# Weighted context as [token, feature] instead of [feature, token] in a gated cross-attention block

## The chip, the cores and the metric

The kernel runs on one core of one Trainium2 chip. The metric is the device time of one execution in microseconds; the time before is the median of three runs. Engine names in the profile: PE is TensorE (PEld its weight loads), DVE VectorE, ACT ScalarE, POOL GpSimd, SP SyncE, which issues most transfers.

## What is computed

Eight sequences (B = 8) of 512 tokens with 256 features attend to 1024 context rows of 192 features each. Per head (4 heads of 32) the 32 largest scores of a token are kept, their softmax is the attention row, and the mean over the heads weighs the context:

```python
Q = (x_text @ Wq).reshape(Bb, Tt, H, DH)
K = (x_vision @ Wk).reshape(Bb, Gg, H, DH)
scores = jnp.einsum('bthd,bghd->bhtg', Q, K) / np.sqrt(DH).astype(np.float32)
topv, topi = jax.lax.top_k(scores, K_TOP)
probs = jax.nn.softmax(topv, axis=-1)
attn = jnp.zeros_like(scores).at[bi, hi, ti, topi].set(probs)
attn_mean = attn.mean(axis=1)
V = x_vision @ Wv
c_t = jnp.einsum('btg,bgd->btd', attn_mean, V)
```

c_t then scales and shifts (FiLM) the normalised tokens ahead of and behind a state-space layer (a long convolution, done as a Fourier transform by matrix products); layer norms, a GELU MLP, and a mixture of a shared expert and one of eight routed experts follow. The kernel folds Wv into the FiLM weights, so that what the attention has to deliver is u = attn_mean @ context, 192 features per token.

## The kernel before

**Tiles.** P = 128, NT = 4 token tiles per batch, NG = 8 groups of 128 context rows, DK = 96 (half of the 192 context features), D = 256. All matrices here are float32. Each batch's context lies in SBUF as `s.cx` [128 rows of a group, 8 groups, 192 features], from a pool with two buffers for that tile, so the load of a batch's context (`prepare`, line 432) waits until the context two batches earlier has been read for the last time.

**Attention** (`attention`, line 907) steps through batch, token tile and pair of heads. A step takes the scores from TensorE (pS), copies them by ScalarE (sc), finds the threshold by VectorE (mn, hi, top), exponentiates, masks and normalises, and GpSimd adds the heads into `acc` [128 tokens, 1024 context rows]. When a token tile's four heads are done, `weighted` (line 871) is left for the next step (`behind`), where it is called after the first half of that step's work.

**`weighted`**, per token tile: eight transposes bring acc to `aT` [context row, group, token] by two banks of PSUM (pa) and two copies by ScalarE. Then for each half k of the features, eight products accumulate over the groups into a third bank (pu): the context's 96 columns are the weights in the array, the tile's 128 tokens stream. The result is [96 features, 128 tokens] for each half, side by side in one bank, and one ScalarE copy takes both halves to `s.uT` [feature, half, token]. `film` (line 1032) later uses uT as the weights of its own products, pfi at the start of `mixed` and pfo at its end.

**Order.** Nothing is issued as it is called. The calls are noted as operations with a modelled cost (`Plan.time`), and `Plan.order` (line 220) simulates the five queues and picks for each engine, among what can begin, the operation with the lowest place in program order. That place is shifted: attention's operations by `LEAD_A` = -100, which puts them behind others, the scores forward again by `LEAD_S` = 300. PSUM banks of the tag "mm" (`bank`, line 397; four of them) and SBUF buffers are granted in program order when one comes free (`grant`, line 243). So a change in one operation's cost, or one more bank, can change the order of everything after it. The streams are interleaved: attention of batch b runs beside `mixed` and `after_mix` of batch b - 1 and the preparation of batch b + 1; routed expert blocks (pxb, pg, pu<-xbT, pyr) are set between. After the last attention tile the last batch's remaining stages and the rest of the expert blocks run alone. The name pu appears twice in the profile: pu<-aT,cx is the weighted context, pu<-xbT,rt_up an expert's product.

**Setting.** `weighted` is called 32 times in the path that runs; a second path for masked rows (`attention_masked`) holds a call too, under a condition that the inputs here don't meet.

Of the kernel before, what the change touches and what calls it, by code (L numbers as in the profile page):

```python
# [12 lines left out]
F32 = mybir.dt.float32  # L13
# [9 lines left out]
P = 128  # L23
# [320 lines left out]
def tile_kernel(ctx: ExitStack, tc: tile.TileContext, a: dict, out: bass.AP):  # L344
# [8 lines left out]
    NE, _, NI = a["L0_ffn_rt_gate"].shape  # L353
    NT, NG, DK = T // P, G // P, DV // 2
# [26 lines left out]
    pk = ctx.enter_context(tc.tile_pool(name="pk", bufs=2))  # L381
# [9 lines left out]
    V, S, GP, TE, SY = (plan.engine(n, e) for n, e in (  # L391
        ("DVE", nc.vector), ("ACT", nc.scalar), ("POOL", nc.gpsimd), ("PE", nc.tensor), ("SP", nc.sync)))
# [4 lines left out]
    def bank(name, pool=ps_mm, tag="mm"):  # L397
        return pool.tile([P, 512], F32, tag=tag, name=name)
# [9 lines left out]
    ident = const.tile([P, P], F32, name="ident")  # L408
# [462 lines left out]
    def weighted(b, s, t, acc):  # L871

        aT = pa.tile([P, NG, P], F32, tag="aT", name=f"aT{b}_{t}")
        for q in range(NG // 4):
            p_ = bank(f"pa{b}_{t}_{q}")
            for i in range(4):
                g = 4 * q + i
                TE.transpose(p_[:, i * P : (i + 1) * P], acc[:, g * P : (g + 1) * P], ident)
            S.copy(aT[:, 4 * q : 4 * q + 4, :].rearrange("p g t -> p (g t)"), p_)
        p_ = bank(f"pu{b}_{t}")  # L880
        for k in range(2):
            for g in range(NG):
                TE.matmul(p_[:DK, k * P : (k + 1) * P], s.cx[:, g, k * DK : (k + 1) * DK],
                          aT[:, g, :], start=(g == 0), stop=(g == NG - 1))
        S.copy(s.uT[:DK, :, t * P : (t + 1) * P],
               p_[:DK, : 2 * P].rearrange("p (k t) -> p k t", k=2))

# [19 lines left out]
    def attention(states):  # L907
# [5 lines left out]
        for k, (b, t, h0) in enumerate(steps):  # L913
# [72 lines left out]
            if h0 + 2 == H:  # L986
                behind = partial(weighted, b, s, t, acc)
# [3 lines left out]
    def attention_masked(b, s):  # L991
# [3 lines left out]
        for t in range(NT):  # L995
            acc = pk.tile([P, G], F32, tag="acc", name=f"acc{b}_{t}")
            for h in range(H):
# [29 lines left out]
                else:  # L1027
                    V.scalar_tensor_tensor(acc, sc, sm[:, 3:4], acc, ALU.mult, ALU.add)
            weighted(b, s, t, acc)


# [396 lines left out]
    p_ = bank("p_ok")  # L1428
# [4 lines left out]
    with tc.If(rows_ok < P):  # L1433
# [10 lines left out]
        for b in range(B):  # L1444
            s = St()
# [51 lines left out]
```

## Time and profile before

| | |
|---|---|
| median of 3 runs | 1786.56 us (1785.48 to 1790.18) |
| the profiled execution | 1792.2 us, span 1790.5 us |
| TensorE busy | 1517.7 us, 85% of the span |
| VectorE busy | 1302.9 us, 73% |
| ScalarE busy | 1154.7 us, 64% |
| GpSimd busy | 929.5 us, 52% |
| mean granted TensorE clock | 0.873 |
| pu<-aT,cx products | 1024 instructions, 116.0 to 1557.9 us, 136.5 us busy |
| first copy to uT, last | 121.3 us, 1558.3 us |

A row of the groups gives the engine and operation, the tile written and those read, for a product the partitions * weight columns, then the shape of the moving operand and the number of instructions; behind the bar the busy time in us and the mean duration of one in ns; behind the next bar the idle time just before, and what ended it. Products are pipelined: a row's mean duration is longer than the distance between two starts. In a busy table each engine has its busy us and the instructions in that stretch; then follow the granted clock (1.00 is full rate), the share of the DMA engines and GB/s. Nearly all instructions carry line 323, the place where the planned order is issued, so groups are told apart by their tiles.

### The profile page before, as it was taken

How to read it: one execution, taken by the hardware profiler on the slowest of the kernel's cores; microseconds unless marked ns; L12 is line 12 of the kernel's file. 1: busy time of each engine (PE TensorE's matmuls, PEld its weight loads, DVE VectorE, ACT ScalarE, POOL GpSimd, SP SyncE). 2: the span in 40 equal slices, each digit the busy share in tenths (PEclk: the TensorE clock that was granted, in tenths of full speed). 3: DMA queues.
4: the chain of work that ended last, by engine and by line, in shares of the span. 5: the costliest groups of instructions: out<-in, count | busy, mean ns of one | idle time of the engine just before them, and what ended most of it. 6: DMA issues, size and time to landing. Idle time of an engine off the chain costs nothing. (4 is left out here: it accounts for less than half of the span.)

```text
span 1790.5 us, 21072 instructions
## 1 busy us (share of the span) xinstructions
PE 1517.7 (85%) x6363; PEld 893.1 (50%) x6363; DVE 1302.9 (73%) x3076; ACT 1154.7 (64%) x2008; POOL 929.5 (52%) x1072
## 2 busy tenths in 40 slices
PE   5365577797998798999889999998999989969995
PEld 2143333344543454474436554654466447637795
DVE  5999977886878697977798889687978798231210
ACT  4778844676747774887578877885788568312321
POOL 5578543445363645565554755574557555432222
PEclk8555677786998799998989999998999899989998
DMA  4000110001200120143103330432033204653592
GB/s 118 0 1 24 33 36 18 12 12 47 64 25 12 47 65 18 36 127 95 56 12 101 89 111 12 130 110 61 12 102 103 80 1 133 206 176 118 162 304 70
DMA packets 101288, 131.67 MB, mean 74 GB/s; under 512 B 9687, under 2 KB 73004, under 8 KB 101166
## 3 DMA queue, kind: packets, MB, share of 16 engines
q1 hardware_dynamic: 93102, 121.05, 21.1%
q0 software_dynamic: 7008, 8.42, 2.6%
q8 instruction: 52, 0.85, 0.2%
q10 hardware_dynamic: 1056, 0.79, 0.2%
q14 instruction: 70, 0.57, 0.1%
HBM read 112.22 MB, written 18.78 MB: 73 GB/s over the span
## 5 line engine op out<-in xcount | busy, mean ns | idle before, releaser
L323 PE MATMUL pS<-kT,qT 32*128 32x512 f32 x512 | 287.7, 748 | 71.0 <-DVE mn L323 60.6
L323 POOL TENSOR_TENSOR acc<-acc,e 128x1024 f32<-128x1024 f32 x96 | 229.1, 2386 | 184.4 <-ACT e L323 181.8
L323 DVE MAX8 top<-mn 128x8 f32<-128x256 f32 (+1 forms) x512 | 276.0, 556 | 11.9
L323 ACT COPY sc<-pS 128x512 f32<-128x512 f32 x256 | 145.6, 584 | 174.3 <-PE pS L323 143.7
L323 DVE SCALAR_TENSOR_TENSOR e<-sc,t,e 128x1024 f32<-128x1024 f32 x128 | 180.9, 1426 | 40.9 <-ACT e L323 40.6
L323 DVE TENSOR_TENSOR mn<-sc,pS 128x512 f32<-128x512 f32 x256 | 165.2, 677 | 36.0 <-PE pS L323 19.9
L323 POOL TENSOR_TENSOR mn<-mn 128x256 int32<-128x256 int32 x128 | 102.5, 801 | 167.5 <-DVE hi L323 166.8
L323 PEld LDWEIGHTS pS<-kT,qT 32*128 32x128 f32 x512 | 76.5, 210 | 204.8 <-DVE mn L323 98.6
L323 ACT ACTIVATE e<-sc,sm 128x1024 f32<-128x1024 f32 x128 | 145.1, 1146 | 15.9 <-POOL acc L323 13.0
L323 ACT ACT_TABLE_LOAD x118 | 151.4, 1283 | 4.1 <-issue 2.0
L323 PE MATMUL pm<-hT,w 128*128 128x512 f32 x256 | 135.9, 668 | 13.5 <-ACT hT L323 13.5
L323 ACT ACTIVATE junk<-sc,sm 128x1024 bf16<-128x1024 f32 x128 | 146.0, 1141 | 1.3
L323 PEld LDWEIGHTS pu<-aT,cx 128*96 128x96 f32 x1024 | 123.2, 169 | 28.6 <-issue 24.1
L323 PE MATMUL pu<-aT,cx 128*96 128x128 f32 x1024 | 136.5, 283 | 0.2 <-ACT aT L323 0.2
L323 PE MATMUL am<-w,ga 128*128 128x256 f32 x512 | 129.1, 398 | 6.1 <-ACT ga L323 6.1
L323 PEld LDWEIGHTS am<-w,ga 128*128 128x128 f32 x512 | 96.9, 196 | 51.4 <-issue 27.6
L323 POOL TENSOR_TENSOR yf<-yf,t 128x512 f32<-128x512 f32 (+1 forms) x80 | 85.9, 1112 | 46.1 <-DVE t L323 45.0
L323 ACT ACTIVATE e<-e,sm 128x1024 f32<-128x1024 f32 x96 | 108.5, 1147 | 1.7 <-DVE sm L323 1.6
L323 POOL TENSOR_TENSOR mn<-mn,hi 128x256 int32<-128x256 int32 x128 | 104.8, 819 | 8.0
L323 DVE MATCH_REPLACE8 mn<-top,mn 128x256 f32<-128x256 f32 x256 | 104.6, 409 | 0.0
L323 PEld LDWEIGHTS pm<-hT,w 128*128 128x128 f32 x256 | 52.1, 213 | 79.2 <-issue 54.2
L323 DVE TENSOR_REDUCE hi<-mn 128x256 f32<-128x512 f32 x128 | 87.9, 687 | 0.0
(303 smaller groups left out, 3073.5 us busy)
## 6 DMA issues: line engine op xcount, KB each, us to landing
w<-in_L_xattn_W_dram SPq DMA_DIRECT2D x32, 512.0 KB
rt_gate<-in_L_ffn_rt_gate_dram SPq DMA_DIRECT2D x30, 512.0 KB
rt_up<-in_L_ffn_rt_up_dram SPq DMA_DIRECT2D x30, 512.0 KB
rt_down<-in_L_ffn_rt_down_dram SPq DMA_DIRECT2D x30, 512.0 KB
cx<-in_ctx_dram SPq DMA_DIRECT2D x7, 768.0 KB
xtab<-zt SPq DMA_DIRECT2D x8, 642.5 KB
xt<-in_x_dram SPq DMA_DIRECT2D x8, 512.0 KB
xo<-in_x_dram SPq DMA_DIRECT2D x8, 512.0 KB
```

What stands on the lines that cost most here:

```text
L323: o.fn()
```

## The change

The products of `weighted` exchange their operands: the tile's attention weights aT [context row, token] become the weights in the array (128 columns), and all 192 features of the context stream at once, so that one chain of eight products gives u as [token, feature] in one bank. ScalarE copies u to SBUF (a new tile of 192 columns with one buffer). Two transposes then turn the two halves of 96 features into a further bank (put), and the copy to `s.uT` is as before. The eight transposes of acc and their copies stay.

```diff
             S.copy(aT[:, 4 * q : 4 * q + 4, :].rearrange("p g t -> p (g t)"), p_)
+
         p_ = bank(f"pu{b}_{t}")
+        for g in range(NG):
+            TE.matmul(p_[:, : 2 * DK], aT[:, g, :], s.cx[:, g, : 2 * DK], start=(g == 0), stop=(g == NG - 1))
+        u = pk.tile([P, 2 * DK], F32, tag="u", name=f"u{b}_{t}", bufs=1)
+        S.copy(u, p_[:, : 2 * DK])
+        p_ = bank(f"put{b}_{t}")
         for k in range(2):
-            for g in range(NG):
-                TE.matmul(p_[:DK, k * P : (k + 1) * P], s.cx[:, g, k * DK : (k + 1) * DK],
-                          aT[:, g, :], start=(g == 0), stop=(g == NG - 1))
+            TE.transpose(p_[:DK, k * P : (k + 1) * P], u[:, k * DK : (k + 1) * DK], ident)
         S.copy(s.uT[:DK, :, t * P : (t + 1) * P],
                p_[:DK, : 2 * P].rearrange("p (k t) -> p k t", k=2))
```

## The prediction

> **What bounds the kernel now.** First the page's busy times and granted clock, then the busy table for three stages that I chose: filter set-up beside the first attention tiles, the steady part, and the tail after the last attention tile.
>
> ```profile
> PE 1517.7 (85%) x6363; PEld 893.1 (50%) x6363; DVE 1302.9 (73%) x3076; ACT 1154.7 (64%) x2008; POOL 929.5 (52%) x1072
> ```
>
> ```profile
> core 0: us, PE busy (x) PEld busy (x) DVE busy (x) ACT busy (x) POOL busy (x), PEclk, DMA share, GB/s
> 100.00:500.00 400.00, 300.52 (x1275) 162.12 (x1276) 325.98 (x707) 274.92 (x463) 216.02 (x197) 0.73 0.09 29
> 500.00:1560.00 1060.00, 981.56 (x3878) 563.73 (x3877) 854.20 (x2104) 769.06 (x1334) 597.99 (x724) 0.94 0.23 71
> ```
>
> From 500 to 1560 us TensorE is busy 93% of the time and no other engine is above 81%: the steady part is TensorE's queue plus its waits. From 100 to 500 VectorE leads (81%) and the clock is granted 0.73. The longest waits of TensorE in the steady part:
>
> ```profile
> PE pc L323 <- DMA cx<-in_ctx_dram: 15.9, 3, 6.2
> PE pm L323 <- ACT hT L323: 12.8, 6, 5.0
> PE pyr L323 <- DVE ger L323: 11.0, 7, 3.1
> PE hT_p L323 <- ACT hh L323: 10.2, 5, 3.8
> ```
>
> All of its waits there add up to about 78 us. So work taken from TensorE counts, unless one of these waits grows by as much. Then the groups that the change touches, or that price what it adds:
>
> ```profile
> L323 PE MATMUL pu<-aT,cx 128*96 128x128 f32 x1024 | 136.5, 283 | 0.2 <-ACT aT L323 0.2
> L323 PEld LDWEIGHTS pu<-aT,cx 128*96 128x96 f32 x1024 | 123.2, 169 | 28.6 <-issue 24.1 <-ACT aT L323 2.2 <-ACT junk L323 1.0
> L323 PE MATMUL pc<-ident,cx 128*96 128x128 f32 x128 | 24.0, 338 | 33.5 <-DMA cx<-in_ctx_dram 33.5
> L323 ACT COPY uT<-pu 96x256 f32<-96x256 f32 x32 | 11.6, 363 | 31.4 <-PE pu L323 31.4
> L323 ACT COPY ktime<-pz 32x128 f32<-32x128 f32 x32 | 8.1, 253 | 10.3 <-PE pz L323 10.1
> ```
>
> A float32 product is two instructions here (32 tiles x 16 products = 512, and 1024 rows), a transpose is one (pc, 128 of them). Means overlap, so costs are taken from starts in TensorE's timeline: at full clock 32 instructions of pu run from 1087.29 to 1090.78, 3.49 us, 109 ns each. Eight of pm with 512 columns take 3.43 us (timeline, 1626.37 to the next row at 1629.80): 429 ns, 0.84 ns a column. A pu instruction is thus its 128 columns (107 ns) and 2 ns more; the weight load is hidden.
>
> **The change, part by part.**
>
> *Products.* Removed per tile: 32 x 109 = 3.49 us. Added: 8 products x 2 instructions x 192 columns x 0.84 = 16 x 161 = 2.58 us. Fewer columns stream, because 192 columns fill the moving side where 96 of 128 array columns were used. Weights now have 128 columns instead of 96, but there are half as many loads; pg with 128-column weights and 128 moving columns takes 1.79 us for 16, 112 ns, so a 128-column load already hides under 112 ns and will under 161. I count 0 for it; if the cover failed, 3 ns x 16 x 32 = 1.5 us in all.
>
> *Two transposes per tile,* nearest row pc (same 96 x 128 shape): 2 x 109 = 0.22 us. TensorE net: 3.49 - 2.58 - 0.22 = 0.69 us saved per tile at full clock, double at half clock.
>
> *The copy of u,* PSUM to SBUF, 128 x 192, on ScalarE: between the ktime copy (253 ns, 128 columns) and the uT copy (363, 256 columns): 0.31 us, 32 times, 9.8 us. The uT copy stays. No activation table changes with a copy.
>
> *One more bank of the four* (put) per tile, and a new wait: the transposes wait for the copy of u, which waits for the last product. Behind it in ScalarE's queue stand the copies of sc and hh, in TensorE's whatever the planner places after put.
>
> *Where 0.69 us goes, tile by tile.* I listed every pu burst with the next wait of TensorE. Four kinds.
>
> (B) The burst is the last reader of a context buffer, and the next context's load waits for it:
>
> ```profile
> 859.45 2.21 PE L323 MATMUL pu<-aT,cx 128*96 128x128 f32 x18
> 866.70 1.86 PE L323 MATMUL pc<-ident,cx 128*96 128x128 f32 x8 [5.05 <-DMA cx<-in_ctx_dram]
> ```
>
> ```profile
> 861.69 0.37 SPq L439 DMA_DIRECT2D cx<-in_ctx_dram  x1
> ```
>
> pu ends at 861.6, the load is issued at 861.69, TensorE stands 5.05 us. Here the products end 0.91 us sooner, and copy and transposes fall into the wait: the whole 0.91 counts. Three such in the steady part (waits at 678, 867, 1229), two early (293 at half clock, so 1.8; 495): 4 x 0.91 + 1.8 = 5.4 us.
>
> (C) The burst fills the time of the layer norm ahead of the MLP:
>
> ```profile
> 714.11 2.13 PE L323 MATMUL pu<-aT,cx 128*96 128x128 f32 x18
> ...
> 720.97 0.46 PE L323 MATMUL pu<-aT,cx 128*96 128x128 f32 x2
> 722.22 2.16 PE L323 MATMUL hT_p<-ident,hh 128*128 128x128 f32 x8 [0.79 <-ACT hh L323]
> ```
>
> hh depends on VectorE, GpSimd and ScalarE, not on pu: a shorter pu only lengthens the 0.79. Six tiles (530, 714, 905, 1087, 1270, 1450): 0.
>
> (D) The next wait is for VectorE (116, 178, 242, 337, 411, 596): 0, late next is the same VectorE step. The last tile (1554) is followed by 5 us of pfi that it does not feed: 0.
>
> (A) The other 14, among them 656, 771, 958, 1128, 1171, 1311 and 1355: TensorE goes on with work whose later waits start from TensorE's own products (ger after pg and pu), so they move along: 14 x 0.69 = 9.7 us.
>
> Gain 15.1. Against it: the copy of u may stand ahead of hh in the 6 (C) places, 6 x 0.31 = 1.9, and ahead of copies of sc on which pS waits (TensorE's pS waits 43.0 us at the load and 8.8 at the product for them): I take half of the other 26 tiles at 0.31 x 0.5, 2.0. The bounds are 0 and 9.8, all copies laid end to end; I stay low because ScalarE is at 73% in the steady part. The bank: bounds below zero (a new order may also suit) and 0.65 us per tile (see rivals); I take 1. Sum: -15.1 + 1.9 + 2.0 + 1 = -10 us.
>
> **A rule against the change.** The busy table around the (C) place at 1087, granted clock in the third column from the end:
>
> ```profile
> 1088.00:1093.00 5.00, 4.66 (x31) 3.35 (x29) 4.72 (x18) 2.08 (x4) 4.48 (x8) 1.00 0.34 105
> 1096.00:1100.00 4.00, 3.57 (x4) 1.51 (x5) 4.00 (x6) 3.57 (x10) 0.40 (x2) 0.50 0.00 0
> ```
>
> TensorE waits 1.10 us at 1093.76 and 0.68 at 1096.43, and the grant falls from 1.00 to 0.50. The Trainium skill, page "TensorE: Matmul & The Clock Gate", section "Why this matters for your kernels", says that gaps up to about 3 us keep the clock, and longer ones halve it. By the rule the change would push one (C) gap over the edge (2.56 us at 912 to 3.25), and a 3.4 us stretch at half rate, the shortest that this trace's clock record has, would cost 1.7 us. By the trace gaps of 1.1 us are already followed by half rate, so nothing is left to lose: 0. Here measurement and page differ; I take 0 and keep 6 x 1.7 = 10 us as the outer bound, should all six (C) places lose another stretch.
>
> **The sum.** The profiled execution took 1792.2 us (span 1790.5, 1.7 around it); it becomes 1782. It lies 5.6 above the median of the runs, 1786.56; I take those 5.6 as this execution's own and expect them again, so the forecast for the median is 1786.6 - 10 = 1776 (rounded down).
>
> **Rivals.**
>
> *Full gain.* Every tile counts, as TensorE's busy share suggests: 32 x 0.69 / 0.87 mean clock = 25 us, 1761. Against it: the (C) and (D) rows. Chance 0.08.
>
> *Hidden.* The (A) bursts too are fillers, done at low priority (attention's lead of -100 puts them behind everything ready), and VectorE at 81% takes over: only (B) is left, 5.4 less the copies' 3.9: 1785. Chance 0.20.
>
> *Slower: a fourth bank per tile.* pa, pa, pu and put are asked for one after the other from a pool of four, granted in program order. pa starts at 703 and pu ends at 721: put's bank is held idle for most of that, and two banks instead of three are left for py, pm, pg, pxb and the rest. If each tile costs one more round trip through an evacuation, as the 0.65 us that pm waits for hT at 1460, this is 32 x 0.65 = 21 us: 1797. It decides from 0.35 us per tile ((10 + 1) / 32, the 1 being what the sum already holds) on; slower than 0.3% from 0.5. For it: these bursts live long. Against it: TensorE's four longest waits name no bank. A planner that reorders everything by a changed cost adds to both sides. Chance 0.30.
>
> **How the numbers follow.** Forecast's case (5 to 20 us less) 0.42. Faster by over 0.3% (5.4 us, about what a measurement of this kernel tells from no change): 0.42 + 0.08 = 0.50; within 0.20; slower 0.30. The forecast's own range is 1767 to 1781. The range for 8 in 10 has to reach the slower case: 1763 (most of the full gain) to 1798.
>
> **What would show it.** pu with 512 products of 128 x 192 and about 136.5 x 2.58 / 3.49 = 101 us busy; put with 64 transposes, about 8 us; a copy u<-pu at 310 ns. Right: the three waits pc<-cx no longer, TensorE's steady waits grow by about 6 x 0.7 = 4 us at hT_p and pm. Wrong: the steady waits grow by 15 us or more (hidden), waits of pm, pg, pxb or py for ScalarE's evacuations appear (banks), the copy of u takes over 0.4 us, or a 192-column instruction takes much over 161 ns.

## The result, and the profile after

The changed kernel takes 1817.99 us (median of 6 runs, 1816.42 to 1827.78) against 1787.15 for the kernel before (6 runs): the ratio is 1.0185, with a 95% interval of 1.017 to 1.020. It is slower by some 31 us, where 10 us less were forecast. The profiled execution took 1816.97 us, its span is 1815.3. (In the table of experiments below a ratio leaves disturbed executions out; the one there was, of one_bank at 1860.84 us, is still in that run's median.)

The page's first part, then the groups that the change touched (columns as before):

```profile
PE 1514.6 (83%) x5915; PEld 876.2 (48%) x5915; DVE 1304.5 (72%) x3076; ACT 1166.2 (64%) x2043; POOL 942.4 (52%) x1072
```

```profile
L323 PE MATMUL pu<-cx,aT 128*128 128x192 f32 x512 | 104.0, 347 | 1.3 <-ACT aT L323 1.3
L323 PE MATMUL put<-ident,u 128*96 128x128 f32 x64 | 14.7, 307 | 0.8 <-ACT u L323 0.8
L323 ACT COPY uT<-put 96x256 f32<-96x256 f32 x32 | 11.8, 367 | 27.9 <-PE put L323 27.8
L323 ACT COPY u<-pu 128x192 f32<-128x192 f32 x32 | 10.2, 319 | 28.0 <-PE pu L323 27.9
```

The new instructions cost about what was worked out: pu is busy 104 us instead of 136.5 (101 was expected), the copy of u takes 319 ns (310). So the products did become cheaper, and still TensorE's busy time fell by only 3.1 us in all. The granted clock explains this in part. The mean is 0.863 of a span of 1815.3 against 0.873 of 1790.5. The trace's clock record has no grants but 1.00 and 0.50, so that is 2 x 0.137 x 1815 = 497 us at half rate after and 455 before, 42 us more. Of TensorE's busy time 320 us lie in such stretches after and 303 before, so the estimate for the products is half of 17, some 8 us; 21 us would be lost only if TensorE were busy in all of the 42. The rest is idle time. TensorE's idle time in the groups adds up to 284.3 us after and 255.9 before, +28.4; with -3.1 busy this is the span's +25.

The longest waits of TensorE in the steady part (500 to 1560 us), in the changed kernel:

```profile
PE pc L323 <- DMA cx<-in_ctx_dram: 24.4, 5, 5.9
PE hT_p L323 <- ACT hh L323: 22.0, 6, 5.7
PE pS L323 <- ACT sc L323: 20.4, 11, 8.9
PE pS L323 <- DVE mn L323: 8.2, 9, 3.4
PE pyr L323 <- DVE ger L323: 7.3, 4, 2.9
```

The third line is what stands out. In the same stretch before it was this:

```profile
PE pS L323 <- ACT sc L323: 4.7, 4, 2.3
```

The first two grew too, from 15.9 and 10.2 us. All waits there add up to 99 us (1060 less 960.6 busy) instead of 78, more than the 15 us of growth that the prediction named as a sign of being wrong. pm's wait for hT, one of the signs of its bank rival, fell from 12.8 to 3.2 us. The instructions of pS and sc have not been changed. What did change around them is their order: of ScalarE's 2008 instructions before, with the numbers in the tiles' names taken off, only 1185 keep their order among each other in the changed kernel's trace. The planner was given other costs, another number of operations and one more bank, and laid out the whole kernel anew.

### The profile page after: what moved, and what is told of

Read it like the earlier page. It is cut to its first block, busy times and chain, and to the rows that moved or that the text cites. A ratio compares the mean times of both kernels' runs of the same rounds, so it can differ in the third digit from the quotient of the medians.

```text
span 1815.3 us, 20202 instructions
## 1 busy us (share of the span) xinstructions
PE 1514.6 (83%) x5915; PEld 876.2 (48%) x5915; DVE 1304.5 (72%) x3076; ACT 1166.2 (64%) x2043; POOL 942.4 (52%) x1072
## 5 line engine op out<-in xcount | busy, mean ns | idle before, releaser
L323 PE MATMUL pS<-kT,qT 32*128 32x512 f32 x512 | 294.8, 754 | 96.5 <-DVE mn L323 63.5
L323 PE MATMUL am<-w,ga 128*128 128x256 f32 x512 | 124.4, 387 | 5.5 <-ACT ga L323 5.5
L323 POOL TENSOR_TENSOR yf<-yf,t 128x512 f32<-128x512 f32 (+1 forms) x80 | 90.6, 1170 | 64.1 <-DVE t L323 62.9
L323 PE MATMUL pu<-cx,aT 128*128 128x192 f32 x512 | 104.0, 347 | 1.3 <-ACT aT L323 1.3
L323 PEld LDWEIGHTS pu<-cx,aT 128*128 128x128 f32 x512 | 90.5, 202 | 23.1 <-issue 17.7
L323 POOL TENSOR_TENSOR mn<-mn,hi 128x256 int32<-128x256 int32 x128 | 96.2, 752 | 8.4
L323 PE MATMUL pfi<-wf,uT 96*128 96x512 f32 (+1 forms) x128 | 77.7, 730 | 8.5 <-DVE xm L323 8.0
```

The lines of the kernel that those rows point to most:

```text
L323: o.fn()
```

## The experiments

Theories: *order* (the new instructions are worth the forecast -10 us, and the new layout of everything else costs some 40); *bank* (the fourth bank starves the others, the prediction's slower rival); *work* (the copy of u and the wait pu, u, put, uT cost more than they save wherever they stand). Later two finer ones about what in a layout costs: *queue* (ScalarE standing at a copy whose product is not done) and *scores* (scores taken too far ahead).

| run | what it is | median us | ratio to before, 95% |
|---|---|---|---|
| old_order | the change's work in the order of before | 1777.98 | 0.9954, 0.9939 to 0.9970 |
| one_bank | the change without its fourth bank | 1835.41 | 1.0266, 1.0245 to 1.0287 |
| plan_only | before, products assumed cheaper | 1834.51 | 1.0275, 1.0256 to 1.0294 |
| before_leads | before, scores' lead 320 | 1791.85 | 1.0026, 1.0008 to 1.0044 |
| before_leada | before, attention's lead -95 | 1802.41 | 1.0112, 1.0047 to 1.0177 |
| after_leada60 | change, attention's lead -60 | 1810.21 | 1.0133, 1.0110 to 1.0155 |
| old_order_late | old_order, transposes later | 1806.03 | 1.0099, 1.0076 to 1.0122 |
| early_copy | before, copy to uT earlier | 1804.58 | 1.0100, 1.0063 to 1.0137 |
| hold_long | old_order, transposes and copy to uT held back | 1784.08 | 0.9972, 0.9958 to 0.9987 |
| hold_short | old_order, held less | 1782.02 | 0.9970, 0.9957 to 0.9983 |
| slow_products | change, products assumed dearer | 1801.83 | 1.0073, 1.0050 to 1.0096 |
| after_held | change, copies held back | 1823.51 | 1.0191, 1.0171 to 1.0211 |
| after_leads200 | change, scores' lead 200 | 1796.81 | 1.0062, 1.0045 to 1.0078 |
| after_leads250 | change, scores' lead 250 | 1815.98 | 1.0138, 1.0095 to 1.0181 |
| after_leads400 | change, scores' lead 400 | 1826.49 | 1.0226, 1.0209 to 1.0243 |

**Same work, old order.** The planner notes the operations of before; only what each of the 17 issues per tile is replaced:

```diff
+        n0 = len(plan.ops)
         for k in range(2):
             for g in range(NG):
                 TE.matmul(p_[:DK, k * P : (k + 1) * P], ...
         S.copy(s.uT[:DK, :, t * P : (t + 1) * P], ...
+        ops = plan.ops[n0:]
+        for o in ops[: 2 * NG]: o.fn = lambda: None
+        for g in range(NG): ops[g].fn = partial(nc.tensor.matmul, p_[:, : 2 * DK], aT[:, g, :], s.cx[:, g, : 2 * DK], ...)
+        ops[11].fn = partial(nc.scalar.copy, u_, p_[:, : 2 * DK])
+        ops[15].fn = turn    # both transposes, into columns 256 to 511 of the same bank
+        ops[16].fn = partial(nc.scalar.copy, s.uT[...], p_[:DK, 2 * P :]...)
```

> The whole work of the change (16 product instructions of 192 columns, the copy of u, two transposes, the copy to uT per tile), but issued in the order that the planner gave the kernel before, instruction for instruction; the transposes go into free columns of pu's own bank. Order theory (the new instructions are as cheap as the sum said, the time was lost because the planner laid out everything else anew): 1776 us or a little less, at most 1781. Work theory (the copy of u and the wait pu, u, put, uT cost more than they save wherever they stand): stays at 1800 to 1818. Bank theory (a fourth bank per tile starves the others): also 1776, since there is no fourth bank here.

Measured: 1777.98, 9 us less than before. Outside these products every queue is issued in the order of before; in the trace all 2008 of ScalarE's instructions keep it, and the 32 added copies bring no further table load (118, as before). The busy table and the groups of this run:

```profile
100.00:500.00 400.00, 295.09 (x1167) 154.61 (x1168) 328.58 (x710) 276.43 (x472) 217.62 (x199) 0.73 0.10 29
500.00:1560.00 1060.00, 969.88 (x3576) 547.58 (x3576) 856.67 (x2109) 774.61 (x1360) 597.33 (x726) 0.94 0.25 75
```

```profile
L323 PE MATMUL pu<-cx,aT 128*128 128x192 f32 x512 | 99.2, 341 | 0.2 <-ACT aT L323 0.2
L900 PE MATMUL pu<-ident,u__96 128*96 128x128 f32 x64 | 13.5, 292 | 13.5 <-ACT u__96 L323 13.0
L323 PE MATMUL pc<-ident,cx 128*96 128x128 f32 x128 | 23.2, 330 | 23.5 <-DMA cx<-in_ctx_dram 23.5
```

The clock of these two stages is that of before, 0.73 and 0.94, where the change in its own order shows this:

```profile
100.00:500.00 400.00, 293.02 (x1152) 153.44 (x1152) 331.92 (x723) 279.00 (x474) 219.97 (x202) 0.71 0.09 27
500.00:1560.00 1060.00, 960.63 (x3466) 539.43 (x3467) 845.13 (x2076) 773.30 (x1351) 599.19 (x698) 0.92 0.23 67
```

In the same 1060 us the change in its own order gets 3466 instructions through TensorE and in the old order 3576. Work theory falls: the same products, copies and transposes gain in one order and lose in another, 40 us apart. (This run has no fourth bank, and one fixed buffer for u; the next runs take the bank up.)

**No fourth bank.**

```diff
-        p_ = bank(f"put{b}_{t}")
         for k in range(2):
-            TE.transpose(p_[:DK, k * P : (k + 1) * P], u[:, k * DK : (k + 1) * DK], ident)
+            TE.transpose(p_[:DK, (k + 2) * P : (k + 3) * P], u[:, k * DK : (k + 1) * DK], ident)
```

> The change with the transposes in columns 256 to 511 of pu's own bank, so that no fourth bank is asked for; everything else, the planner's costs too, as in the change. Bank theory: 1776 to 1787, most of the loss is gone. Order theory: no fixed value; the planner again lays out everything anew, so anything from 1780 to 1820, and most of the queue differs from before as it does in the change. Work theory: stays at 1810 to 1818.

Measured: 1835, slower than with the fourth bank. So the loss does not need the bank, and bank theory falls as its cause. What the bank itself costs is not shown, since without it the planner made yet another layout.

**The kernel before, planned differently.**

```diff
                 TE.matmul(p_[:DK, k * P : (k + 1) * P], s.cx[:, g, k * DK : (k + 1) * DK],
                           aT[:, g, :], start=(g == 0), stop=(g == NG - 1))
+                if plan.noting:
+                    plan.ops[-1].cost *= 0.723
```

> The kernel before, with all its instructions; only the cost that the planner assumes for each of the 16 products is multiplied by 0.723, the ratio of what it assumes for the change's products (2.91 us a tile) to those of before (4.02). No copy of u, no transposes, no further bank. Order theory: slower than before by about half or more of what the change lost, 1797 to 1820, though no instruction is added. Bank and work theories: 1787, as before, within 0.3%.

Measured: 1834.51, with not one of the program's own instructions added or removed: beyond the expected 1820, and more than the whole loss of the change. So a changed assumed cost is enough for a loss of this size. Up to 850 us its copies to uT lie within 6 us of those of before, then they fall behind (the last begins at 1601.7 us, before at 1558.3). The change loses elsewhere: its fifth copy to uT begins at 355.3 us against 342.2, its last at 1581.6. One reservation: the cost that this run's planner assumes is too low for the products that run, while the change's planner was given a fair one. ScalarE's wait at the copy to uT, 31.4 us before, became

```profile
ACT uT L323 <- PE pu L323: 58.7, 24, 9.5
```

and the new order needs nine more of ScalarE's table loads (127 instead of 118, 11.5 us busy). So this run shows how far an order can move the time, not what the change's order costs. Two plain nudges of the leads, in the kernel before and in the change, show how wide the layouts scatter:

```diff
-LEAD_A, LEAD_P, LEAD_S = -100, -100, 300
+LEAD_A, LEAD_P, LEAD_S = -100, -100, 320    # before_leads; -95, -100, 300 in before_leada
```

> The kernel before, nothing changed but the planner's lead of the scores, 320 operations in place of 300: the same instructions in another order. Order theory (the order of before is a good one among its neighbours, and any new layout loses): slower, 1795 to 1830. Rival (only the cheaper products or the fourth bank mislead the planner, other nudges are harmless): within 0.3% of 1787.

> The kernel before, nothing changed but the lead of attention's operations, -95 in place of -100: the same instructions in another order. Order theory: slower, 1795 to 1830. Rival: within 0.3% of 1787.

> The changed kernel, its instructions as they are, with the lead of attention's operations at -60 in place of -100. Order theory: a different time from the change's 1818, by more than 5 us either way, and a lower one is likelier, 1795 to 1810, since 1818 is only one draw among orders. Work and bank theories: 1818 within 0.3%, since the copy, the wait and the fourth bank are all still there.

(The last is the change with -60, -100, 300.) Measured: 1792, 1802 and 1810. The first missed its range on the low side (1795 was the lowest expected) and lies at 0.26%, under the 0.3% that the prediction took for no change: here the rival held, that other nudges are harmless. The second and third are as the order theory had them. None of the three other layouts that the kernel before was run in beat its own (1787 against 1792, 1802, 1834). How its settings were once chosen is not on record.

**One pair moved within the old order.**

```diff
-            ops[11].fn = partial(nc.scalar.copy, u_, p_[:, : 2 * DK])
-            ops[15].fn = turn
+            ops[8].fn = partial(nc.scalar.copy, u_, p_[:, : 2 * DK])
+            ops[16].fn = partial(turn, s.uT[...], ...)    # transposes, then the copy to uT
```

> As the run with the order of before, but the copy of u is put into ScalarE's queue halfway through the products' old places and the two transposes go into TensorE's queue only where the copy to uT stood, some instructions later, since TensorE waited 13 us in all at the transposes for the copy of u there. Order theory: 4 to 10 us below that run, 1768 to 1774. Work theory: no gain, 1778, the wait only moves to ScalarE.

A miss: 1806 instead of 1768 to 1774. In the trace the transposes now begin 3.1 us (median) behind the last product, 1.0 us in old_order. ScalarE's waits at the two copies, first in old_order, then in this run:

```profile
ACT u__96 L323 <- PE pu L323: 24.1, 13, 9.3
...
ACT uT L323 <- PE pu L900: 3.9, 7, 0.8
```

```profile
ACT u__96 L323 <- PE pu L323: 49.8, 24, 9.1
...
ACT uT L901 <- PE pu L900: 29.3, 18, 5.7
```

28 us became 79, and TensorE's 13.0 us at the transposes became 0.8. ScalarE's instructions run in the order in which they are issued (all 2008 in old_order's trace stand as before), so everything behind the copy waits too. The 28 us lost here (26 by the ratios), with one copy and two transposes moved, suggested the queue theory; the run does not tell the copy's earlier place from the transposes' later one. To try it in the kernel before, five products and the copy were issued early:

```diff
+            ops = plan.ops[n0:]
+            early = [o.fn for o in ops[11:]]
+            ops[11].fn = lambda: [f() for f in early]
+            for o in ops[12:]: o.fn = lambda: None
```

> The kernel before in its own order, with its own instructions; only the last five of the 16 products per tile and the copy to uT are issued together where the twelfth product stood, so that the copy stands up to some 1.3 us earlier in ScalarE's queue. Queue theory (what a new layout costs above all is ScalarE standing at the head of its queue for a pu that is not done; the run with the late transposes had 79 us of it and 1806, the run with the order of before 28 and 1778): ScalarE's wait at the copy rises from 31 to 50 or more, and the time by about half of that, 1796 to 1812. Rival (these waits are idle time of an engine with slack, the loss comes from other places of a new layout): 1787 within 0.3%.

Measured: 1804.58, and the wait at the copy to uT rose from 31.4 us to this:

```profile
ACT uT L891 <- PE pu L891: 58.0, 28, 10.1
```

So 27 us more of waiting went with 18 us more of time. It could as well be the five products taken ahead of other work on TensorE; the run does not separate the two.

**Held back.** The operations are issued in the planned order, but the transposes and the copy to uT are kept until the plan's clock has gone on by 1.0 and 1.8 us (hold_long, with the copy of u at `ops[13]`) or 0.6 and 1.2 us (hold_short):

```diff
+            plan.hold[ops[15].i], plan.hold[ops[16].i] = 1.0, 1.8
```

> The work of the change in the order of before, with the copy of u two products' places later than in the first such run, the transposes held back by 1.0 us of planned time in TensorE's queue and the copy to uT by 1.8 us in ScalarE's. Queue theory: ScalarE's waits at the two copies fall below the 28 us of that run and TensorE's at the transposes below 13; 1765 to 1776. Rival: no better than 1778, since the pair then waits elsewhere or frees its bank later.

> As the long hold, with 0.6 and 1.2 us and the copy of u where the first such run had it. Queue theory: between that run and the long hold, 1768 to 1778. Rival: 1778 or above.

Measured: 1784 and 1782, both above what the queue theory hoped and as its rival had them. The two waits of ScalarE add up to 40 and 41 us, since the held transposes now stand behind other products. The intervals of both overlap old_order's, so 28 us and 1778, 41 and 1782, 40 and 1784 cannot be told apart; only old_order_late, 79 and 1806, stands clear. That these waits set the time is suggested within the old order, not shown.

**In the change's own order.** Two runs ask whether the same waits (27.9 and 27.8 us in the changed kernel) are what its layout loses by. One makes the planner leave more room (`plan.ops[-1].cost *= 1.382` at the eight products), the other holds the copy of u and the transposes back by 0.8 us and the copy to uT by 2.0.

> The changed kernel, instruction for instruction its work, with the planner's assumed cost of the eight products raised to what it assumed for the 16 of before, 4.02 us a tile. Queue theory: the planner leaves more room before the copy of u, ScalarE's waits at the two copies fall from 56 us, and the time falls below 1818, to 1795 to 1812. Order theory without that (any new layout is another draw): 1800 to 1840, with no tie to those waits; the planner's own total, 15 us longer than for the change, would say 1833.

> The changed kernel with its own layout; only the copy of u and the transposes are held back by 0.8 us of planned time in their queues, and the copy to uT by 2.0 us. From the pairs of runs with one layout (28 us of waiting at the copies and 1778, 41 and 1782, 79 and 1806; 31 and 1787, 58 and 1805) a us of such waiting costs 0.55 to 0.65 us. Queue theory as the whole cause: the 56 us fall to about 30 and the time goes to about 1780 to 1790. Queue theory as a part: the time falls by 0.6 for each us of wait that goes, 1798 to 1808, and the rest of the loss stays with the layout. Rival (those waits are no cause here): 1818 within 0.3%.

Measured: 1801.83 and 1823.51. The first came out as the queue theory had it, though the waits fell only from 56 to 50 us (in an execution of 1810.66 us, the slowest of its six), too little to account for 16 us. The second speaks against it: the waits fell to 39 us and the time did not fall.

```profile
ACT u L334 <- PE pu L338: 20.2, 10, 5.5
...
ACT uT L334 <- PE put L334: 18.8, 7, 9.3
```

The run with attention's lead at -60 speaks against it too. It has no more of these waits than old_order, and took 1810 us:

```profile
ACT u L323 <- PE pu L323: 16.9, 15, 2.5
...
ACT uT L323 <- PE put L323: 10.0, 12, 3.1
```

As the cause of the change's loss the queue theory falls. One more candidate was in the change's trace, ScalarE's waits at the copies of the scores for VectorE to be done with e, since the buffers of sc are reused (31.1 us, 10.5 before):

```profile
ACT sc L323 <- DVE e L323: 31.1, 15, 8.3
```

> The changed kernel with the lead of the scores at 200 operations in place of 300. Scores theory (scores taken too far ahead block ScalarE): its waits at the copies of the scores for VectorE's use of e fall from 31 us to 15 or less, TensorE's for those copies from 33 to 15 or less, and the time to 1785 to 1805. Draw theory (no single wait, each layout another draw, before's among the best): 1800 to 1835.

> The changed kernel with the lead of the scores at 250. Scores theory: between 200 and the change, 1795 to 1812, with the two waits in between. Draw theory: 1800 to 1835, without that order.

> The changed kernel with the lead of the scores at 400. Scores theory: slower than 1818, 1822 to 1840, with more of both waits. Draw theory: 1800 to 1835, either side.

Measured, by lead: 200 gives 1797, 250 gives 1816, 300 (the change) 1818, 400 gives 1826. The median rises with the lead, as the scores theory said, but 250 lies above the range it gave and cannot be told from 300, and the waits do not carry it: for VectorE's e they are 13.9, 20.3, 31.1 and 11.2 us, for TensorE at those copies 17.8, 20.1, 32.7 and 27.7. At 400 the time is highest and the first wait lowest.

**Where the time lies.** A wait is only one part of what an order changes. The row of the score products, busy time and idle time before it taken together, tells the layouts apart better. Before, old_order, the change, the change with lead 200, plan_only:

```profile
L323 PE MATMUL pS<-kT,qT 32*128 32x512 f32 x512 | 287.7, 748 | 71.0 <-DVE mn L323 60.6
L323 PE MATMUL pS<-kT,qT 32*128 32x512 f32 x512 | 285.1, 743 | 76.2 <-DVE mn L323 63.9
L323 PE MATMUL pS<-kT,qT 32*128 32x512 f32 x512 | 294.8, 754 | 96.5 <-DVE mn L323 63.5
L323 PE MATMUL pS<-kT,qT 32*128 32x512 f32 x512 | 270.3, 760 | 82.8 <-DVE mn L323 64.8
L323 PE MATMUL pS<-kT,qT 32*128 32x512 f32 x512 | 313.3, 776 | 76.5 <-DVE mn L323 66.8
```

The sums are 359, 361, 391, 353 and 390 us. From old_order to the change the row takes 30 us more, of 42 between the two spans. All seven runs of the change's work with spans from 1808 to 1824 us have 376 to 396; the old order and its variants, lead 200 and the kernel before, but for plan_only, have 353 to 365. With lead 200 the row's busy time falls by 24.5 us against the change and the span by 21. So the larger part of the change's loss lies at the scores. That is a place and not yet a cause: no run moved the scores alone, and in before_leada, early_copy and old_order_late the time rose with this row unchanged.

## Why the prediction was wrong, point by point

- **The prices: right.** pu is busy 104.0 us (101 expected) and the copy of u takes 319 ns (310). A 192-column product with 128-column weights needed no extra time for the loads: at full clock the distance from start to start is 163 ns in old_order (161 expected). Only put was mis-sized: 14.7 us busy for "about 8 us", which counted 109 ns from start to start, where the row holds the whole duration of a pair, 307 ns for one.
- **The sum of -10: near for the edit alone, in part by luck.** With the order of before it is -9. But the terms were not confirmed one by one. Waits of pc for the context fell from 33.5 to 23.5 us, 10 where (B) had 5.4; and TensorE waited 13.0 us at the transposes for the copy of u, a wait that the prediction named and for which it counted nothing. The (C) places kept their waits (hT_p 19.0 to 19.2 us, pm 13.5 to 12.7); the growth of 4 us did not show. And these are figures of two executions that lie 17 us apart (spans of 1790.5 and 1773.2), not 9.
- **The step that failed** is the one that let the rest of the kernel stand: the tile-by-tile list of where 0.69 us goes took each neighbour of pu from the trace of before, and the planner was one sentence, that reordering "adds to both sides". So the new order was put at nothing in the sum, though a changed cost, as the section on the kernel's order says, can move everything after it. In its place the runs show 40 us, four times the edit's gain: 1777.98 in the order of before, 1817.99 in the planner's new one. To both sides it did not add in any layout tried: three others of the kernel before are slower or the same, and the change's instructions in seven layouts of the planner's own (1797 to 1835, one_bank among them) are all slower than in the borrowed one. The range's upper end of 1798 had only the bank to reach for.
- **The rival on the slower side** had the sign but not the mechanism: 1797 by a fourth bank. Without that bank the kernel takes 1835. The sign of *hidden* did appear, steady waits grown by 21 us; in the old order, with the same bursts between the same neighbours, they grew by 12 (to 90) and the gain was there.
- **The clock rule** was weighed at 0, at most 10 us. For the edit alone the profiled run has a higher clock than before (0.878, 0.873), but it was the second fastest of its six; by the medians the old order has 0.871 and the kernel before beside it 0.876, 15 us more at half rate and so up to 8 us lost, inside that bound. In the new order half-rate time grew by 42 us, by the estimate above some 8 us of the loss and at most 21. That the clock is not what decides is seen with lead 200: 506 us at half rate, more than the change's 497, and 21 us faster.

Open: why the scores take longer in the new layout, and what makes up the rest of the 40 us. Holding the copies back did not return it, less lead of the scores returned about half (1797), and no single wait follows the times of all the runs. It was not tried to move one engine's order while keeping the others'.

The fastest version found is the change's work in the order of before, 1777.98 us, 0.5% below the kernel before.

## What to carry to other kernels

Where one planner orders every queue, an edit has two prices: its instructions, which a profile gives well, and the new order of everything else, which the profile of before does not give at all. Measure the first by itself, by issuing the new work in the old order; the difference to the changed kernel is the second. How far orders scatter can be learnt ahead of any edit, by nudging the planner of the old kernel: here two nudges of a lead cost 6 and 16 us and a false cost 47, against a gain of 9 to be had. If the two prices differ in sign, keep the order and change the work, or search the planner's settings again for the new work before judging it (one setting tried here returned 21 us). And compare whole rows, busy and idle, and not waits alone: an order also changes what an engine's own work takes.

## What was not expected of the hardware

Two of pS's instructions keep TensorE for as long as four that stand together (in the program, the products of two heads):

```profile
1082.30 1.12 PE L323 MATMUL pS<-kT,qT 32*128 32x512 f32 x2
1083.35 1.12 PE L323 MATMUL pfo<-wf,uT 96*128 96x512 f32 x2
1084.41 1.13 PE L323 MATMUL pS<-kT,qT 32*128 32x512 f32 x4
1085.46 1.99 PE L323 MATMUL pfo<-wf,uT 97*128 97x512 f32 x4
```

From the start of the group to the next product it is 1.05 us for both (kernel before, full clock). So an order that splits them costs TensorE some 1.05 us each time, and this is busy time, not a wait. With lead 200 there are 48 such groups of four and 103 of two, in the change 30 and 146; 18 more of four are worth some 19 us, an estimate, of the 24.5 us that the row lost. plan_only has 12 and 170, the kernel before 28 and 150. Between the kernel before and the change they do not differ enough to matter.

A copy and two transposes moved by a few places in in-order queues went with 28 us (1778 to 1806), though ScalarE, which they make wait, is busy only 64% of the span. TensorE's granted clock went down with it, from 0.871 to 0.861 in the medians of the runs: 458 and 503 us at half rate, so up to 23 us of products' time. These runs do not show whether the waits lowered the clock or something else in the move did.
